# Dilated attention and a binary convolution on one core: four tiles for the weighted values, two softmax temporaries in one tile, two output tiles, and a subtraction moved within its slice

## The chip, the cores and the metric

The kernel runs on one core of a Trainium2 chip. The metric is the device time of one execution in microseconds (us). Engines are named as the profile names them: PE is TensorE (PEld its weight loads), DVE VectorE, ACT ScalarE, POOL GpSimd, SP SyncE, which here issues nearly all DMAs. Every compute engine and every DMA queue takes its instructions in one fixed order.

## The reference

The input x is 16 images of 56 x 56 pixels with 384 channels, float32. Two layers follow each other, each with a residual:

```python
def _gn(v, G=32, eps=1e-5):            # group norm over an image, 32 groups of 12 channels
    ...
# layer 0: three groups of 128 channels with dilation 1, 2, 3; 4 heads of 32 channels in each
q, k, v = split(einsum('bchw,oc->bohw', _gn(x), w_qkv))
attn = softmax(einsum('bgdn,bgdkn->bgnk', q, unfold(k)) * 32 ** -0.5)   # 9 neighbours of a pixel
y = einsum('bgnk,bgdkn->bgnd', attn, unfold(v))
x = x + einsum('bhwc,oc->bhwo', y, w_proj) + b_proj
# layer 1: depthwise 3x3 convolution with the signs of w
x = x + conv(_gn(x), sign(clip(w, -1, 1)))
```

So each pixel looks at nine neighbours at a distance of 1, 2 or 3, for 12 heads, and the result goes through a projection. The second layer needs the statistics of a whole image of the first.

## The kernel before

**Tiling.** An image is cut into 7 chunks of 8 rows (448 pixels); 112 chunks in all. Channels lie on the 128 partitions, pixels along the free dimension, so that one product is a [128, 448] float32 matmul and one [128, 3, 448] tile holds three neighbours. A tile of w takes 3 x 448 x 4 = 5376 bytes of each partition.

**Three plans.** plan_a loads a chunk of x, turns it to channels (L423), takes statistics and writes it to DRAM (xd). plan_b is the attention of chunk m. plan_c convolves the chunk ten steps earlier and writes the output. The pieces of these plans are put into a table with at(slice, order, piece): a chunk advances by 9 slices, and within a slice the pieces stand in the order SOFTMAX, SCORE, STATISTICS, CONVOLVE, WEIGH, QUERY, SPREAD, QKV, PROJECT, STAGE_A, STAGE_C, NORM, LOADS. The table is issued from front to back. The framework then fixes the order of each engine's instructions when it builds the program. It takes what is ready, and the issued order is a priority: in the trace, work of later slices stands ahead of earlier work in places. It also inserts every wait.

**The attention of a chunk**, with the names that the text below uses (t0 is 9m):
- project (L464) makes k and v in slices before and during the chunk, query the three q. The rows that chunks share are copied by small DMAs (L478, L479).
- score(i), slices t0 to t0+8: VectorE multiplies q with three neighbours of k into a tile t (L517), and TensorE adds over the channels of a head with a matrix of ones into ps (L502), in three bursts a chunk.
- softmax_1 (t0+9): ScalarE copies ps into the tile sT (L534), TensorE turns it to pixels (L537), VectorE subtracts the maximum (L540, L541), ScalarE takes the exponential (L542). softmax_2 (t0+10): VectorE's sum (L546), reciprocal, and product (L548).
- softmax_3 to 5: the float32 weights are split into three bf16 terms. ScalarE copies the first (L556, the tile e). GpSimd subtracts it from the weights into the tile rest (L560, softmax_4, slice t0+11), copies the second term (L564) and subtracts for the third (L565, softmax_5, slice t0+12). turn_weights is a transposing DMA into aT (L570) and needs all three.
- weigh(i), slices t0+14 to t0+22, i = 3g + ky: TensorE spreads the weights of three neighbours over the channels into pb_a (L583, one buffer of PSUM), VectorE multiplies them with v into a tile of w (L590), and for ky = 1 and 2 GpSimd adds that tile to the first of its group (L598). After ky = 2 GpSimd adds the three parts into y (L601, L602).
- out_project(j), slices t0+24 on (L616): it needs all three y.

Tiles of w come from the pool w_p, which has three; so a group's first tile stays in use until L602, and each of the other two until its own L598. The pool also gives out tiles for some chunks of the first image, and in every second chunk of the last image for the convolution's input (z_last).

**The convolution of a chunk** puts two thirds of the channels on TensorE (L711) and one third on ScalarE and GpSimd: the normalised tile zg (L740), nine products on ScalarE (L762), two big adds on GpSimd (L768, of [128, 1344]) and three small ones (L773, L773, L776). turn(s), four times a chunk, turns 112 pixels back (L783); ScalarE copies them into a tile osb (L788), and SP writes that to the output (L791). The pool o_p has three tiles of osb (1536 bytes of a partition each).

Of the kernel before, what the change touches and what calls it, by code (L numbers as in the profile page):

```python
# [8 lines left out]
F32 = mybir.dt.float32  # L9
# [8 lines left out]
P = 128  # L18
HEADS = 4
# [5 lines left out]
SUB = 112  # L25
# [3 lines left out]
NPAD = 32  # L29
# [6 lines left out]
def dilated_attention_then_binary_conv(  # L36
# [30 lines left out]
    PX = ROWS * W  # L67
    NCH = H // ROWS
    NSUB = PX // SUB
# [78 lines left out]
    xn_p = ctx.enter_context(tc.tile_pool(name="xn_p", bufs=3))  # L148
    xr_p = ctx.enter_context(tc.tile_pool(name="xr_p", bufs=1))
    t_p = ctx.enter_context(tc.tile_pool(name="t_p", bufs=4))  # L150
    w_p = ctx.enter_context(tc.tile_pool(name="w_p", bufs=3))
    y_p = ctx.enter_context(tc.tile_pool(name="y_p", bufs=4))
    s_p = ctx.enter_context(tc.tile_pool(name="s_p", bufs=1))
    a_p = ctx.enter_context(tc.tile_pool(name="a_p", bufs=2))
    x1_p = ctx.enter_context(tc.tile_pool(name="x1_p", bufs=2))
    xg_p = ctx.enter_context(tc.tile_pool(name="xg_p", bufs=2))
    m_p = ctx.enter_context(tc.tile_pool(name="m_p", bufs=3))
    o_p = ctx.enter_context(tc.tile_pool(name="o_p", bufs=3))


    kv = []
# [231 lines left out]
    def at(when, order, piece):  # L393

        pieces.setdefault((when, order), []).append(piece)
# [50 lines left out]
    def plan_b(m, t0):  # L446

        b, c = divmod(m, NCH)
        had = {}
# [75 lines left out]
        def by_neighbour(ap):  # L525
            return ap.rearrange("p s (o k) -> p s o k", o=NTAP)

        def over_neighbours(ap):
            return ap.unsqueeze(2).to_broadcast([SUB, NSUB, NTAP, GH])

        def softmax_1():

            sT = s_p.tile([P, PX], F32, tag="sT", name="sT")
            nc.scalar.copy(sT, had.pop("ps")[:, :PX])  # L534
            pt = ps_mt.tile([P, 512], F32, tag="mt", name="pt_s")
            for s in range(NSUB):
                nc.tensor.transpose(pt[:SUB, s * P : (s + 1) * P], sT[:, s * SUB : (s + 1) * SUB], permf)  # L537
            pt4 = pt[:SUB].rearrange("p (s v) -> p s v", s=NSUB)[:, :, :NR]
            mx = s_p.tile([SUB, NSUB, GH], F32, tag="mx", name="mx")
            nc.vector.reduce_max(mx, by_neighbour(pt4).rearrange("p s o k -> p s k o"), axis=AX.X)  # L540
            nc.vector.tensor_tensor(by_neighbour(weights), by_neighbour(pt4), over_neighbours(mx), ALU.subtract)  # L541
            nc.scalar.activation(weights, weights, AF.Exp, scale=SCALE)  # L542
# [13 lines left out]
            nc.scalar.copy(term[0], e8)  # L556

        def softmax_4():
            had["rest"] = rest = s_p.tile([SUB, NSUB * NPAD * HEADS], F32, tag="rest", name="rest")
            nc.gpsimd.tensor_tensor(rest.rearrange(EIGHTS, k=8), e8, term[0], ALU.subtract)  # L560

        def softmax_5():
# [70 lines left out]
        for i in range(9):  # L633
            at(t0 + i, SCORE, lambda i=i: score(i))
        at(t0 + 9, SOFTMAX, softmax_1)
        at(t0 + 10, SOFTMAX, softmax_2)
        at(t0 + 11, SOFTMAX, softmax_3)
        at(t0 + 11, PROJECT, softmax_4)
        at(t0 + 12, SOFTMAX, softmax_5)
        at(t0 + 12, LOADS, turn_weights)  # L640
        for i in range(9):
# [182 lines left out]
    SOFTMAX, SCORE, STATISTICS, CONVOLVE, WEIGH, QUERY, SPREAD, QKV, PROJECT, STAGE_A, STAGE_C, NORM, LOADS = range(13)  # L824
# [43 lines left out]
    for m in range(N):  # L868
        plan_a(m, start_a(m))
        plan_b(m, STEP * m)  # L870
        plan_c(m, STEP * (m + 10))
# [31 lines left out]
```

## Time and profile before

| | |
|---|---|
| median of 3 runs | 5359.44 us (5357.7 to 5360.04) |
| the profiled execution | 5363.24 us |
| its span, first to last instruction | 5361.5 us |
| mean granted TensorE clock | 0.978 |
| TensorE idle from 500 to 5000 us | 4500 less 4404.4 busy: 95.6 us |
| L598, GpSimd's add of w | 672 times, 3080 ns |
| L590, VectorE's product into w | 1008 times, 1543 ns |
| L560 / L564 / L565 on GpSimd | 112 times each, 1154 / 607 / 1159 ns |
| aT from issue to landing | 112 times, 4.0 us |
| output parts | 420 DMAs of 168 KB from tiles osb |

Busy time says how full an engine is over the whole span. Where an engine stands idle, the trace names what ended the wait: "PE ps L502 <- DVE t L517" means that TensorE's matmul into ps began when VectorE's product t was done. "L590 [1.93 <-POOL w L598]" means that VectorE had been idle for 1.93 us until GpSimd's add ended. "issue" is time in which the engine waited for nothing that the profile shows.

### The profile page before, as it was taken

What the parts mean: (1) busy time and instruction counts of PE and PEld (TensorE: products, weight loads), DVE (VectorE), ACT (ScalarE), POOL (GpSimd) and SP (SyncE); (2) the same over time, 40 slices, a digit from 0 to 9 for tenths busy, and PEclk for the clock granted to TensorE, in tenths of its full rate; (3) what the DMA queues carried; (4) which work ended last, traced back from release to release, by engine and by line L of the source; (5) the groups of instructions that cost most, each with busy time, mean ns of one, the idle gap of its engine ahead of it and who ended that gap; (6) DMA issues with size and microseconds to landing.
All of it is one profiled execution on the core that took longest, in us unless ns stands there. A gap on an engine that the chain in (4) does not pass through costs nothing. (4 is left out here: it accounts for less than half of the span.)

```text
span 5361.5 us, 75511 instructions
## 1 busy us (share of the span) xinstructions
PE 5146.8 (96%) x26885; PEld 2339.3 (44%) x26885; DVE 4173.9 (78%) x4125; ACT 2310.0 (43%) x4077; POOL 4254.0 (79%) x2950
## 2 busy tenths in 40 slices
PE   8999999999999999999999999999999999999976
PEld 4444444444444444444444444444444444444433
DVE  5887887778778777887878877777887878877764
ACT  3213444444444444444444444444434444444434
POOL 2777888888888887878888888888888888788881
PEclk8999999999999999999999999999999999999986
DMA  6434555555555555555555555565555555544455
GB/s 192 135 108 113 166 161 162 161 155 162 155 164 157 152 159 162 166 155 161 161 154 166 147 161 161 160 165 154 165 158 155 162 147 164 146 135 134 130 135 154
DMA packets 811631, 825.62 MB, mean 154 GB/s; under 512 B 360307, under 2 KB 801014, under 8 KB 811254
## 3 DMA queue, kind: packets, MB, share of 16 engines
q1 hardware_dynamic: 803270, 808.79, 54.7%
q10 hardware_dynamic: 7984, 12.00, 0.7%
q8 instruction: 213, 3.49, 0.3%
q14 instruction: 164, 1.34, 0.1%
HBM read 466.41 MB, written 231.21 MB: 130 GB/s over the span
## 5 line engine op out<-in xcount | busy, mean ns | idle before, releaser
L598 POOL TENSOR_TENSOR w<-w 128x1344 f32<-128x1344 f32 x672 | 2069.9, 3080 | 587.3 <-DVE w L590 544.6
L590 DVE TENSOR_TENSOR w<-pb_a,v 128x1344 f32<-128x1344 f32 x1008 | 1555.7, 1543 | 327.4 <-PE pb_a L583 213.9
L517 DVE TENSOR_TENSOR t<-pq,k 128x1344 f32<-128x1344 f32 x1008 | 1536.2, 1551 | 252.0 <-PE pq L464 251.6
L464 PE MATMUL pkv<-xn,wqkvT 128*128 128x448 f32 x3924 | 1567.6, 548 | 0.4 <-DVE xr L619 0.4
L464 PEld LDWEIGHTS pkv<-xn,wqkvT 128*128 128x128 f32 x3924 | 718.0, 190 | 670.7 <-issue 644.9
L464 PE MATMUL pq<-xn,wqkvT 128*128 128x448 f32 x1962 | 858.8, 573 | 0.0
L616 PE MATMUL po<-y,wprojT 128*128 128x448 f32 x2016 | 832.8, 549 | 23.9 <-POOL y L602 18.4
L697 ACT ACTIVATE z<-z,mrz 96x448 f32<-96x448 f32 x840 | 578.2, 751 | 631.6 <-DMA z<-x1d 371.5
L768 POOL TENSOR_TENSOR m<-m 128x1344 f32<-128x1344 f32 x210 | 640.1, 3048 | 147.4 <-ACT m L762 143.1
L502 PE MATMUL ps<-t,sel 128*32 128x448 f32 x6048 | 663.5, 548 | 45.0 <-DVE t L517 44.3
L762 ACT ACTIVATE m<-zg,ktap 128x448 f32<-128x448 f32 x945 | 555.5, 659 | 8.6 <-POOL xg L776 1.7
L616 PEld LDWEIGHTS po<-y,wprojT 128*128 128x128 f32 x2016 | 375.6, 191 | 381.5 <-issue 339.5
L711 PE MATMUL pc<-z,kdiag 96*32 96x440 f32 (+1 forms) x5040 | 517.5, 544 | 6.1 <-POOL z L699 4.4
L464 PEld LDWEIGHTS pq<-xn,wqkvT 128*128 128x128 f32 x1962 | 353.0, 194 | 330.3 <-issue 330.3
L583 PE MATMUL pb_a<-aT,spread 24*128 24x448 bf16 x3024 | 369.9, 360 | 82.6 <-DMA aT<-e 60.6
L602 POOL TENSOR_TENSOR y<-y,w 128x448 f32<-128x448 f32 x336 | 381.2, 1134 | 16.4
L601 POOL TENSOR_TENSOR y<-w 128x448 f32<-128x448 f32 x336 | 381.3, 1135 | 13.7
L619 DVE SCALAR_TENSOR_TENSOR xr<-po,bias,xr 128x448 f32<-128x448 f32 x336 | 227.9, 678 | 208.5 <-PE po L616 203.8
L474 ACT COPY v<-pkv 128x448 f32<-128x448 f32 x336 | 176.3, 525 | 493.7 <-PE pkv L464 484.7
L718 DVE TENSOR_TENSOR x<-pc,x 128x448 f32<-128x448 f32 x224 | 139.0, 621 | 310.4 <-PE pc L711 309.3
L583 PEld LDWEIGHTS <-spread 24*128 24x128 bf16 x3024 | 100.3, 91 | 571.1 <-issue 488.5
L474 ACT COPY k<-pkv 128x448 f32<-128x448 f32 x336 | 178.9, 532 | 377.2 <-PE pkv L464 377.2
(132 smaller groups left out, 4278.3 us busy)
## 6 DMA issues: line engine op xcount, KB each, us to landing
z<-x1d SPq DMA_DIRECT2D x570, 224.0 KB, 3.8
xr<-xd SPq DMA_DIRECT2D x112, 672.0 KB, 4.2
x1d<-xr SPq DMA_DIRECT2D x112, 672.0 KB, 3.2
xn<-xd SPq DMA_DIRECT2D x109, 672.0 KB, 4.6
xin<-in_x_dram SPq DMA_DIRECT2D x105, 672.0 KB, 7.2
xd<-xa SPq DMA_DIRECT2D x315, 224.0 KB, 3.3
out_dram<-osb SPq DMA_DIRECT2D x420, 168.0 KB, 3.5
x<-x1d SPq DMA_DIRECT2D x112, 448.0 KB, 8.1
```

What stands on the lines that cost most here:

```text
L464: nc.tensor.matmul(dst[:, :PX], wqkvT[:, cc, o0 : o0 + P], had["xn"][:, cc, :], start=(cc == 0), stop=(cc == NG - 1))
L502: return nc.tensor.matmul(had["ps"][32 * j : 32 * j + 32, :PX], sel[:, s0 : s0 + 32], tk, start=(issued[j] == 1), stop=(issued[j] == len(r ...
L517: nc.vector.tensor_tensor(t.rearrange("p k (r w) -> p k r w", w=W), q3, k3, ALU.mult)
L583: return nc.tensor.matmul(pb[:, kx, :PX].rearrange("p (s n) -> p s n", s=NSUB), spread[rows_of, v % 2, :], had["a"][rows_of, :, v // 8, :] ...
L590: nc.vector.tensor_tensor(w.rearrange("p k (r w) -> p k r w", w=W), pb[:, :, :PX].rearrange("p k (r w) -> p k r w", w=W), three(kv[1][g][m ...
L598: nc.gpsimd.tensor_tensor(w0, w0, w, ALU.add)
L601: nc.gpsimd.tensor_tensor(y, w0[:, 0], w0[:, 1], ALU.add)
L616: nc.tensor.matmul(po[:, :PX], wprojT[:, g, j * P : (j + 1) * P], had[f"y{g}"], start=(g == 0), stop=(g == NG - 1))
L697: nc.scalar.activation(z, z, AF.Identity, bias=mrz[:, j, q, 0:1], scale=mrz[:, j, q, 1:2])
L711: return nc.tensor.matmul(pcr[q * HD : (q + 1) * HD, :, lo:hi], kdiag[:, kx, j * NQ + q, :], rows(set_of(j, q))[:, :, lo + kx - 1 : hi + k ...
L762: nc.scalar.activation(rows(t[:, kx]), zp[:, ky : ky + ROWS, kx : kx + W], AF.Copy, scale=ktap[:, o : o + 1])
L768: nc.gpsimd.tensor_tensor(had["m"], had["m"], t, ALU.add)
```

## The change

The pool of w gets a fourth tile, and the pool of osb goes from three to two. The tile rest loses its own place: it takes the tag sT, of which there is one tile, now of 512 instead of 448 columns; so the turned scores and the rest share it in turns. In bytes of a partition: 5376 more for w, 1536 less for osb, 2048 less for rest, 256 more for sT, 2048 more in all. The piece softmax_4 stays in slice t0+11 but moves from the order PROJECT to SOFTMAX, behind softmax_3 of the same slice. No instruction's work changes.

```diff
-    w_p = ctx.enter_context(tc.tile_pool(name="w_p", bufs=3))
+    w_p = ctx.enter_context(tc.tile_pool(name="w_p", bufs=4))
...
-    o_p = ctx.enter_context(tc.tile_pool(name="o_p", bufs=3))
+    o_p = ctx.enter_context(tc.tile_pool(name="o_p", bufs=2))
...
-            sT = s_p.tile([P, PX], F32, tag="sT", name="sT")
+            sT = s_p.tile([P, NSUB * NPAD * HEADS], F32, tag="sT", name="sT")[:, :PX]
...
-            had["rest"] = rest = s_p.tile([SUB, NSUB * NPAD * HEADS], F32, tag="rest", name="rest")
+            had["rest"] = rest = s_p.tile([P, NSUB * NPAD * HEADS], F32, tag="sT", name="rest")[:SUB]
             nc.gpsimd.tensor_tensor(rest.rearrange(EIGHTS, k=8), e8, term[0], ALU.subtract)
...
-        at(t0 + 11, PROJECT, softmax_4)
+        at(t0 + 11, SOFTMAX, softmax_4)
```

## The prediction

> **What bounds the kernel now.** I read the page's busy line first. One engine is nearly full; the two behind it have a fifth of the span free.
>
> ```profile
> PE 5146.8 (96%) x26885; PEld 2339.3 (44%) x26885; DVE 4173.9 (78%) x4125; ACT 2310.0 (43%) x4077; POOL 4254.0 (79%) x2950
> ```
>
> So the end moves only if TensorE's idle time moves. It sums to some 210 us: 45 before 500 us, 96 in the regular part from 500 to 5000 us (4500 less 4404.4 busy, view by windows), 70 after it. Next comes the view of waits for 500 to 5000 us: who ended TensorE's idle time, and VectorE's (in total us, times, longest).
>
> ```profile
> PE pb_a L583 <- DMA aT<-e: 48.8, 13, 4.0
> PE ps L502 <- DVE t L517: 36.6, 36, 1.5
> PE po L616 <- ACT v L474: 5.2, 8, 2.1
> PE pb_a L583 <- DVE w L590: 3.9, 12, 0.4
> ...
> DVE w L590 <- POOL w L598: 47.8, 35, 3.9
> ```
>
> Two causes make nearly all of it. TensorE waits for the turned weights aT 13 times, once per image. And it waits for VectorE's score products t, 1 us at a time. The last line offers a reason for the second: VectorE itself stands before a product w until GpSimd has finished an addition. The timeline of chunk 48 shows whether the two belong together (start, duration, then what is idle in brackets).
>
> ```profile
> 2311.63 2.37 POOL L773 TENSOR_TENSOR m<-m 128x448 f32<-128x448 f32 x2
> 2314.08 1.14 POOL L776 TENSOR_TENSOR xg<-m,xg 128x448 f32<-128x448 f32 x1
> 2315.17 3.03 POOL L598 TENSOR_TENSOR w<-w 128x1344 f32<-128x1344 f32 x1
> ```
> ```profile
> 2313.72 0.36 PE L583 MATMUL pb_a<-aT,spread 24*128 24x448 bf16 x3
> ...
> 2319.85 0.37 PE L583 MATMUL pb_a<-aT,spread 24*128 24x448 bf16 x3 [0.34 <-DVE w L590]
> ...
> 2322.14 1.33 PE L502 MATMUL ps<-t,sel 128*32 128x448 f32 x12 [1.46 <-DVE t L517]
> ```
> ```profile
> 2315.71 0.59 DVE L541 TENSOR_TENSOR ew<-pt_s,mx 112x432 f32<-112x432 f32 x1
> 2318.24 1.56 DVE L590 TENSOR_TENSOR w<-pb_a,v 128x1344 f32<-128x1344 f32 x1 [1.93 <-POOL w L598]
> 2319.71 0.91 DVE L546 TENSOR_REDUCE sm<-ew 112x48 f32<-112x432 f32 x1
> 2320.54 1.55 DVE L517 TENSOR_TENSOR t<-pq,k 128x1344 f32<-128x1344 f32 x1
> ```
>
> This is one chain. The convolution's adds (L768, L773, L776) stand ahead of L598, so the sum of weigh(2) ends at 2318.2. Only then is one of three tiles of w free for weigh(4), whose input pb_a was ready at 2314.1. Its product starts 1.93 us after VectorE had become free, the sum sm and the product t follow it, and TensorE loses 0.34 and 1.46 us. I went through every such gap in 500 to 5000 us: in 31 gaps before ps (35.5 us) and 12 before pb_a (3.9 us) a wait of a w for L598 lies within the 9 us before. Per image it is weigh(4) of the last chunk and of the first.
>
> **What the Trainium skill says.** Perfetto Trace Analysis, Optimization Strategy: the same gap repeating on the engine that should be saturated can mean that there isn't enough SBUF for the next tile. The trace agrees: the 1.46 us above recurs image after image behind a tile that isn't free. SBUF — State Buffer, Who interferes with whom: a VectorE instruction with two SBUF inputs contends with GpSimd's reads, one with a single SBUF input does not. The trace agrees: L548 (two SBUF inputs) takes 583 to 2611 ns, L590 (one PSUM, one SBUF input) 1482 to 1560. So products w that run earlier, beside GpSimd's adds, should not grow.
>
> **The change, part by part.**
>
> *Fourth tile of w.* No instruction is added. weigh(4) may then start when VectorE is free, at 2316.3; sm's sum follows at 2317.8 (its input, the exponential, was there at 2317.0), t at 2318.6 to 2320.2. TensorE is through with its transposes at 2320.35 (2320.69 less the 0.34), so ps waits for nothing: 1.80 us gained. Summed over the regular part: 35.5 + 3.9 = 39.4 us. From below: the skipped wait returns where GpSimd is late next. That is y into the output projection (L602 of chunk 48 ended 2342.6, its first use comes some 5 us later) and aT. For aT I looked at the landing against the first weigh: in ordinary chunks 11.2 us after the end of the bf16 copy L556, against 13.9 when TensorE gets there, so 2.7 us of slack. TensorE comes 1.8 us earlier, GpSimd's chain 0.9 (its idle time before the sum of weigh(5) at 2324.53): 1.8 us of slack stay. I take the whole 39.4; the lower bound is a half, 20.
> Before 500 us the same pattern is worth 0.3 + 2.4 = 2.7 us. From 5000 to 5230 us 13.1 us of TensorE's gaps stand behind such waits, but GpSimd is busy 204.4 of these 230 us and the two waits for y (10.7 and 7.7 us) come from it; only its own idle time before a sum (2.0 + 0.7 + 1.1 us) can go. I take 3, between 0 and 4. The last image's z_last tiles also come from this pool in every second chunk; the chunks between use the four tiles of t and show the same 3.8 us gap, so the tiles don't set it. I take 0, between -4 and 2.
>
> *The rest in the tile of the turned scores.* It adds two orders: L560 after the transposes of sT, and the next chunk's copy L534 after L565. In chunk 48 the transposes were over at 2313.8, L560 began at 2327.8; L565 ended at 2332.8 and the next L534 began at 2355.8. Slacks of 14 and 23 us: nothing. If they were gone, ScalarE would hold its queue (copies of v, k, xa) for the time missing.
>
> *Two output parts.* ScalarE's copy of part n+2 now waits until part n has landed. The view of the tile osb gives the DMA itself:
>
> ```profile
> DMA to landing us min/median/max: 2.1/3.5/5.3
> ```
>
> Taking each copy's landing (where the trace doesn't link one, 3.5 us after its issue) against the start of the copy two later, the order of before leaves over 0.25 us in every case but two of 418, both near 5213 us (3.0 and 0.3 us), where GpSimd is the bound. Price 0; at most 3.3 us; more only if another order packs three copies closely (below).
>
> *Subtraction first in its slice.* softmax_4 issues one instruction, L560 (1.15 us), and no DMA, so SP's queue is passed by nothing. On GpSimd it moves past what its slice holds between the two places: the convolution's second big add (L768, 3.05 us) and, once per image, L333 and L334 (0.19 + 0.20 us). In the trace L768 has run before that point anyway, and L560 stands ahead of L333. Behind L560 on GpSimd are y's adds and L565, which aT and then TensorE wait for. Nothing in the regular order changes: 0. The bound above is the aT wait. Chunk 44 shows it:
>
> ```profile
> 2098.51 1.13 POOL L773 TENSOR_TENSOR m<-m 128x448 f32<-128x448 f32 x1
> 2099.60 1.13 POOL L601 TENSOR_TENSOR y<-w 128x448 f32<-128x448 f32 x1
> 2100.69 1.15 POOL L560 TENSOR_TENSOR rest<-ew,e 112x512 f32<-112x512 f32 x1
> ...
> 2104.56 1.16 POOL L565 TENSOR_TENSOR e<-rest,e 112x512 bf16<-112x512 f32 x1
> ```
>
> L560's input was ready at 2095.2; it starts 5.5 us later, and TensorE loses 3.96 us. But this L773 belongs to a chunk whose zg was made at 2075 us, and its slice is 4 or more after L560's; it still stands ahead: the order is made when the program is built, by what is ready then, and a place within the slice doesn't make L560 ready sooner. I take 0; up to 48.8 us if the builder places it otherwise; down to a loss of its wait for L556 before a ready add, 1.15 us a chunk at most in the chunks without slack.
>
> The sum: 39.4 + 2.7 + 3 + 0 = 45.1 us. The profiled execution took 5363.24 us (span 5361.5 and 1.7 around it), which gives 5318.1; the median of the runs lies 3.8 below that execution, so 5314.3.
>
> **The rivals.**
> *A. Slower: VectorE runs too far ahead.* With a fourth tile a product w (1.55 us, not interruptible) can be placed ahead of a score product t that TensorE wants sooner. The builder re-makes the whole order. Place: the three bursts of ps in each chunk. Price: up to 1.55 us for each burst hit; at 0.8 us once per chunk, 112 x 0.8 = 90 us, less the 45 gained: 5404. It decides from 45.1 / 0.8 = 56 chunks on. For it: already now TensorE loses 0.2 us before ps in several chunks where no w waited, so VectorE is just in time. Against: pb_a has one PSUM buffer, which limits the lead to one product past TensorE's own order.
> *B. The subtraction gets ahead in the third chunk of each image.* Then the 48.8 us go too: 5314.3 - 48.8 = 5265.5. For it: L560 was ready 5 us before its turn. Against: the readiness argument above.
> *C. Nothing gained.* The two-part output or GpSimd hands the time back: products start earlier, but TensorE then waits for aT or y by the same amount. 5359. Against: the slacks of 1.8 and 5 us.
> That the fourth tile isn't used would show as C too.
>
> **How the numbers follow.** Forecast 0.50 (own range 5298 to 5338), B 0.12, C 0.10, A 0.28. About 0.2% (10.7 us) is what a measurement of this kernel can tell from no change. Faster: 0.50 + 0.12 = 0.62; same 0.10; slower 0.28. The range runs from 5275 to 5405: it leaves out B's centre and the upper half of A, under 0.2 together.
>
> **What would show it.** Right: in 500 to 5000 us the line of w waiting for POOL w falls from 47.8 to under 10 us, ps waiting for t from 36.6 to under 8, pb_a waiting for aT stays near 49; busy times are unchanged. Wrong: ps waiting for t grows (A); aT falls to near 0 (B); aT, y, or ScalarE's osb waiting for its own DMA grows by what ps lost (C).

## The result and the profile after

| | before | after |
|---|---|---|
| median, same chip | 5359.74 us (5357.7 to 5362.44, 4 runs) | 5321.87 us (5315.76 to 5325.16, 4 runs) |
| the profiled execution | 5363.24 us (span 5361.5) | 5322.62 us (span 5320.9) |
| mean granted TensorE clock | 0.978 | 0.980 |
| TensorE busy / idle over the span | 5146.8 / 214.7 us | 5132.4 / 188.5 us |

The change makes the kernel faster: ratio 0.9928, 95% interval 0.9911 to 0.9945, 37.9 us by the medians. The busy line of the page after:

```profile
PE 5132.4 (96%) x26885; PEld 2336.6 (44%) x26885; DVE 4203.7 (79%) x4125; ACT 2312.1 (43%) x4077; POOL 4255.0 (80%) x2950
```

The instruction counts are those of before. TensorE has 14 us less busy time for the same work, which the paragraph on the sum takes up. The view of waits from 500 to 5000 us, TensorE's lines and VectorE's for GpSimd (total us, times, longest):

```profile
PE pb_a L583 <- DMA aT<-e: 50.7, 14, 4.0
PE po L616 <- ACT v L474: 11.7, 17, 2.0
PE po L616 <- POOL y L602: 3.7, 1, 3.7
PE ps L502 <- DVE t L517: 1.5, 7, 0.2
...
DVE w L590 <- POOL m L768: 11.3, 8, 1.4
DVE w L590 <- POOL e L564: 10.8, 12, 0.9
```

VectorE's 47.8 us for "POOL w" are gone, and with them TensorE's 36.6 us for t (1.5 left) and 3.9 us for w. The wait for aT stays; its 14th occurrence, 1.7 us at 4973 us, is one that the shorter kernel brings into the window. Two lines have grown: v on ScalarE from 5.2 to 11.7 us, and one wait for y of 3.7 us, at 500.5 us.

Chunk 48 again, the timeline after, first GpSimd, then VectorE and TensorE:

```profile
2298.08 2.37 POOL L773 TENSOR_TENSOR m<-m 128x448 f32<-128x448 f32 x2
2300.53 1.13 POOL L776 TENSOR_TENSOR xg<-m,xg 128x448 f32<-128x448 f32 x1
2301.61 3.04 POOL L598 TENSOR_TENSOR w<-w 128x1344 f32<-128x1344 f32 x1
```
```profile
2302.35 0.59 DVE L541 TENSOR_TENSOR ew<-pt_s,mx 112x432 f32<-112x432 f32 x1
2302.86 1.55 DVE L590 TENSOR_TENSOR w<-pb_a,v 128x1344 f32<-128x1344 f32 x1
2304.32 0.91 DVE L546 TENSOR_REDUCE sm<-ew 112x48 f32<-112x432 f32 x1
2305.14 1.56 DVE L517 TENSOR_TENSOR t<-pq,k 128x1344 f32<-128x1344 f32 x1
```
```profile
2306.85 1.71 PE L502 MATMUL ps<-t,sel 128*32 128x448 f32 x16
```

GpSimd's order is as before, and L598 still ends late, at 2304.65. But the product L590 starts at 2302.86, 1.8 us ahead of that, because it writes the fourth tile. t follows in time, and the burst into ps has no bracket behind it. TensorE's sequence of matmuls, by line and tile, is the same in both traces from the first to the last of 26885. So the two can be laid over each other, matmul by matmul: after less before is -7 us at 500, but within 0.5 us of nothing both at 480 and at 520, then -12 at 2000, -22 at 3000, -33 at 4000, -41 at 5000 and -41 at the end. The gain grows image by image in the regular part; the start and the tail add nothing.

### The profile page after: what moved, and what is told of

Read it like the earlier page. It is cut to its first block, busy times and chain, and to the rows that moved or that the text cites. A ratio compares the mean times of both kernels' runs of the same rounds, so it can differ in the third digit from the quotient of the medians.

```text
span 5320.9 us, 75544 instructions
## 1 busy us (share of the span) xinstructions
PE 5132.4 (96%) x26885; PEld 2336.6 (44%) x26885; DVE 4203.7 (79%) x4125; ACT 2312.1 (43%) x4077; POOL 4255.0 (80%) x2950
## 5 line engine op out<-in xcount | busy, mean ns | idle before, releaser
L598 POOL TENSOR_TENSOR w<-w 128x1344 f32<-128x1344 f32 x672 | 2071.2, 3082 | 535.1 <-DVE w L590 510.4
L590 DVE TENSOR_TENSOR w<-pb_a,v 128x1344 f32<-128x1344 f32 x1008 | 1555.1, 1543 | 276.6 <-PE pb_a L583 225.3
L616 PE MATMUL po<-y,wprojT 128*128 128x448 f32 x2016 | 841.0, 553 | 44.0 <-POOL y L602 32.1
L768 POOL TENSOR_TENSOR m<-m 128x1344 f32<-128x1344 f32 x210 | 640.2, 3048 | 148.2 <-ACT m L762 144.3
```

The source lines that it names most:

```text
L590: nc.vector.tensor_tensor(w.rearrange("p k (r w) -> p k r w", w=W), pb[:, :, :PX].rearrange("p k (r w) -> p k r w", w=W), three(kv[1][g][m ...
L598: nc.gpsimd.tensor_tensor(w0, w0, w, ALU.add)
L616: nc.tensor.matmul(po[:, :PX], wprojT[:, g, j * P : (j + 1) * P], had[f"y{g}"], start=(g == 0), stop=(g == NG - 1))
L768: nc.gpsimd.tensor_tensor(had["m"], had["m"], t, ALU.add)
```

## The experiments

Each was run beside the kernel before. The theory: the fourth tile makes the whole gain, by taking away VectorE's wait for a tile of w; the other edits only make room for it or do nothing; the wait for aT is a second cost that GpSimd's order makes.

**e1: the change with three tiles of w.**

```diff
-    w_p = ctx.enter_context(tc.tile_pool(name="w_p", bufs=4))
+    w_p = ctx.enter_context(tc.tile_pool(name="w_p", bufs=3))
```

> The changed kernel with three tiles of w again: two output parts, the shared tile and the moved subtraction stay. Theory (the fourth tile is the whole gain, the rest is worth nothing): 5360 us within 6, as before the change; from 500 to 5000 us ps waits for t some 36 us and w for POOL w some 48. Rival (the other edits, which alter the order of the last chunks and ScalarE's queue, bring part of it): below 5350, and with all of it near 5322.

Measured: 5359.52 us, ratio to before 1.0008 (0.9999 to 1.0017). Waits from 500 to 5000 us:

```profile
PE ps L502 <- DVE t L517: 34.3, 35, 1.5
...
DVE w L590 <- POOL w L598: 43.6, 33, 4.0
```

Both waits are back, and with them the whole time. Without the fourth tile the other three edits together are worth nothing. The fourth tile without them was not run, so whether it needs the room that they make is not shown.

**e8: the moved subtraction alone, on the kernel before.**

```diff
-        at(t0 + 11, PROJECT, softmax_4)
+        at(t0 + 11, SOFTMAX, softmax_4)
```

> The kernel before with the moved subtraction alone (softmax_4 with the order SOFTMAX). Theory (the builder's choice rests on what is ready, and the place within the slice changes no engine's order): the ratio to before is 1.000, within 0.001, and pb_a waits for aT 47 to 51 us. Rival (B of the prediction: the subtraction gets ahead of L773 in the third chunk of each image): aT near 10 us and some 5308 us.

Measured: 5360.53 us, ratio 1.0000 (0.9992 to 1.0009). The wait for aT is 49.0 us, as before. Every engine's order is that of before (two weight loads apart), so this run is also a second sample of the same program. Its span is 5351.5 us against 5361.5: one profiled execution tells such a program's time to some 10 us only.

**e3: the change with one output part.**

```diff
-    o_p = ctx.enter_context(tc.tile_pool(name="o_p", bufs=2))
+    o_p = ctx.enter_context(tc.tile_pool(name="o_p", bufs=1))
```

> The changed kernel with one output part instead of two; ScalarE's and SP's order change with it. Set against the changed kernel's own times, each copy but one in two would have to wait up to 5 us for the landing of the part before it (197 of 419 copies, 768 us in all on ScalarE). Theory (with two parts the landing is covered, with one it isn't, and ScalarE's queue then reaches TensorE through the copies of k and v): clearly slower than the changed kernel, 5400 to 5700. Rival (ScalarE has the room, 43% busy, and the order is remade around the waits): within 15 us of 5322; then the number of output parts costs nothing at all in this kernel.

Measured: 5413.17 us, ratio 1.0106 (1.0089 to 1.0122), some 90 us above the kernel after. Waits from 500 to 5000 us, TensorE's and one of ScalarE's:

```profile
PE pb_a L583 <- DVE w L590: 33.4, 30, 2.2
PE po L616 <- ACT v L474: 26.3, 40, 1.7
PE pc L711 <- ACT osb L788: 24.0, 12, 3.2
...
ACT osb L788 <- DMA out_dram<-osb: 424.7, 137, 6.8
```

ScalarE stands until a part has landed, and the copies behind it are late. In the kernel after, ScalarE waits so only once, 4.5 us at 5173 us, in the tail. So two are enough, and one is not.

**e5: three tiles, and the convolution's small adds moved behind the sum.** This asks whether the tile or GpSimd's order was the cause. On the kernel before, with `behind(ins, piece)` issuing a piece so that it stands behind `ins` in its engine's queue:

```diff
-            nc.gpsimd.tensor_tensor(w0, w0, w, ALU.add)
+            second[m, i] = nc.gpsimd.tensor_tensor(w0, w0, w, ALU.add)
...
-            at(t0 + 5 + kx, CONVOLVE, lambda kx=kx: sum_g(kx))
+            at(t0 + 5 + kx, CONVOLVE, lambda kx=kx: behind(second.get((m + 8, 2)) if c >= 5 else None, lambda: sum_g(kx)))
```

> The kernel before, three tiles of w, one edit: in the last two chunks of an image of the convolution (c 5 and 6) the three small adds L773, L773, L776 are issued behind L598 of weigh(2) of the attention's chunk m+8, ahead of which they stood. Orders of TensorE, VectorE and ScalarE stay as before but for the last chunks; GpSimd's alone changes. Theory (the tile of w is late because these 3.5 us of adds stand ahead of L598; a fourth tile only hides that): VectorE's wait for POOL w falls from 47.8 us to under 12, ps waiting for t from 36.6 to under 10, aT stays at 48 to 52; 5319 us (5312 to 5330), as with the fourth tile. Rival (three tiles are too few whatever GpSimd's order, since it is some 80% busy and another add will be late): the waits stay over 25 us and the time is 5340 to 5362.

Measured: 5323.47 us, ratio 0.9928 (0.9912 to 0.9945), the ratio of the change itself.

```profile
PE pb_a L583 <- DMA aT<-e: 50.7, 14, 4.0
PE po L616 <- ACT v L474: 9.3, 12, 2.1
PE ps L502 <- DVE t L517: 1.8, 8, 0.3
...
DVE w L590 <- POOL w L598: 8.7, 4, 3.9
```

The chain of the prediction is shown from its other end: with the 3.5 us of L773, L773 and L776 out of the way of L598, three tiles do what four do. The tile buys patience with an order; the order can be had without the tile.

**e2: the change, with the adds of an image's first chunk of the convolution behind L565.** This is what rival B would have brought.

```diff
-            nc.gpsimd.tensor_tensor(term[2], r8, term[1], ALU.subtract)
+            third[m] = nc.gpsimd.tensor_tensor(term[2], r8, term[1], ALU.subtract)
...
-            at(t0 + 5 + kx, CONVOLVE, lambda kx=kx: sum_g(kx))
+            at(t0 + 5 + kx, CONVOLVE, lambda kx=kx: behind(third.get(m + 9) if c == 0 else None, lambda: sum_g(kx)))
```

> The changed kernel, with the three small convolution adds (L773 twice, L776) of each image's first chunk held behind L565 of the chunk in whose slices they fall; TensorE's and VectorE's order stay. Theory (aT is late once per image because 3.4 us of convolution adds and the sum of weigh(5) stand ahead of L560 and L565): TensorE's wait for aT falls from 50.7 us to 10 or less from 500 to 5000 us, some 3.3 us in each of 15 images, and the time from 5322 to 5275 (5265 to 5290). Rival 1 (the held adds make the convolution's output or y late instead): aT falls but the time stays above 5305. Rival 2 (aT is late through its DMA or SP's queue, not through GpSimd's order): aT stays near 50 and the time near 5322.

Measured: 5272.7 us (5269.0 to 5275.65), ratio 0.9844 (0.9829 to 0.9859): the fastest version of the study, 85 us below before. Waits, and GpSimd in chunk 44:

```profile
PE po L616 <- ACT v L474: 21.8, 27, 1.5
PE pb_a L583 <- DMA aT<-e: 10.4, 14, 1.8
```
```profile
2068.57 1.18 POOL L560 TENSOR_TENSOR rest<-ew,e 112x512 f32<-112x512 f32 x1
2069.69 1.15 POOL L601 TENSOR_TENSOR y<-w 128x448 f32<-128x448 f32 x1
...
2072.44 1.17 POOL L565 TENSOR_TENSOR e<-rest,e 112x512 bf16<-112x512 f32 x1
2073.55 2.38 POOL L773 TENSOR_TENSOR m<-m 128x448 f32<-128x448 f32 x2
```

L773 now stands behind L565. The wait for aT falls by 40.3 us, v takes 10.1 of them back, and yet the span falls by 53.6 us (5320.9 to 5267.3). The rest is busy time of TensorE, 23 us less of it, and goes with the clock (below).

**e6 and e9: is the fourth tile needed for that?** e6 puts e2's edit on the kernel before; e9 puts the edits of e2 and e5 there, both with three tiles.

> The kernel before, three tiles of w, with the edit of e2_sums_behind alone: the adds L773, L773, L776 of an image's first chunk of the convolution issued behind L565 of chunk m+9. Theory (the two waits are in different chunks of an image and have nothing to do with each other): the same 49 us as it gave with four tiles, 5357 - 49 = 5308 us (5300 to 5318); pb_a waiting for aT falls from 48.8 to some 10, ps waiting for t stays at 33 to 38, the ratio is 0.991. Rival (they share GpSimd's slack, so the adds put off come to lie ahead of an L598 that has only three tiles): the wait of VectorE for POOL w grows over 60 us and the time is 5325 to 5350.

Measured: 5326.09 us, ratio 0.9933 (0.9918 to 0.9948), the rival's range.

```profile
PE ps L502 <- DVE t L517: 46.0, 45, 1.5
PE po L616 <- ACT v L474: 20.6, 21, 2.4
PE pb_a L583 <- DMA aT<-e: 11.9, 14, 1.8
...
DVE w L590 <- POOL w L598: 98.0, 57, 4.1
```

The wait for aT goes, but VectorE's wait for a tile doubles: the adds put off now stand ahead of an L598 of the third chunk. TensorE pays 9.4 us of it before ps, and its wait for v grows by 15.4 us (5.2 to 20.6) besides.

> The kernel before, three tiles of w, with both edits: those of e5_order_three and of e2_sums_behind (sums of c 5 and 6 behind L598 of chunk m+8's weigh(2), sums of c 0 behind L565 of chunk m+9). Theory (e6 fell short because the adds put off come to lie ahead of an L598 in the third chunk, a gap of 1.07 us before ps once in each of 13 images that only a fourth tile hides): ps waiting for t is 12 to 18 us, aT some 10 us, VectorE's wait for POOL w 40 to 60 us, and the ratio to before is 0.987 (0.9855 to 0.9885), some 14 us over e2_sums_behind. Rival (the two orders together leave no late tile, three are as good as four): the ratio of e2_sums_behind, 0.984 to 0.9854, and ps waiting for t under 6 us.

Measured: 5286.9 us, ratio 0.9859 (0.9844 to 0.9873).

```profile
PE ps L502 <- DVE t L517: 13.8, 19, 1.1
PE pb_a L583 <- DMA aT<-e: 12.9, 14, 1.8
...
DVE w L590 <- POOL w L598: 59.8, 27, 4.1
```

The ratio, ps and VectorE's wait lie in the theory's intervals, the last just so. A gap of some 1.1 us before ps in the third chunk recurs in 10 images of the trace. So the fourth tile does all that e5's order does, and where e2's order is used it seems to be worth more: 12 us less wait before ps than in e9 (2.0 against 13.8), 8 us by the ratios, whose intervals overlap.

**e4: y's adds of the last three chunks on VectorE**, aimed at the waits for y after 5000 us.

```diff
-                nc.gpsimd.tensor_tensor(y, w0[:, 0], w0[:, 1], ALU.add)
-                nc.gpsimd.tensor_tensor(y, y, w0[:, 2], ALU.add)
+                (nc.vector if m >= N - 3 else nc.gpsimd).tensor_tensor(y, w0[:, 0], w0[:, 1], ALU.add)
+                (nc.vector if m >= N - 3 else nc.gpsimd).tensor_tensor(y, y, w0[:, 2], ALU.add)
```

> The changed kernel with the adds into y (L601, L602) of the last three chunks on VectorE instead of GpSimd: 18 adds of 1.13 us leave GpSimd. Theory (the fourth tile brings nothing after 5000 us because GpSimd bounds the last three chunks): TensorE's wait for y falls from 28.5 us there to under 12 and the time by 8 to 18 us, to 5304 to 5314. Rival (the end is set by the loads of z_last and TensorE's lower clock): within 4 us of 5322.

Measured: 5339.73 us, ratio 0.9967 (0.9957 to 0.9978), about 20 us above the kernel after. Both expectations missed. VectorE's and TensorE's waits from 4900 us on:

```profile
DVE y L601 <- POOL w L598: 36.6, 8, 9.2
```
```profile
PE pb_a L583 <- DVE w L590: 31.7, 10, 6.3
PE po L616 <- DVE y L602: 17.6, 2, 10.0
```

The add needs GpSimd's last L598. On GpSimd's own queue that order costs nothing; on VectorE's, the next products w and t are queued behind a wait of up to 9.2 us. The adds themselves are longer there too: the 18 take 22.0 us, where 0.61 us each, the shortest of them, would make 11. How the loss divides between the two, this run doesn't show.

**e7 and e10: the copies of v.** They are what grew in e2. Here is ScalarE, and then TensorE, in the last chunk of an image, in the kernel after:

```profile
3610.81 2.72 ACT L697 ACTIVATE z<-z,mrz 96x448 f32<-96x448 f32 x4 [7.01 <-DMA out_dram<-osb]
3614.12 0.81 ACT L740 ACTIVATE zg<-xg,mr 128x504 f32<-128x504 f32 x1 [0.59 <-DMA xg<-x1d]
3614.96 4.03 ACT L762 ACTIVATE m<-zg,ktap 128x448 f32<-128x448 f32 x7
3618.89 0.52 ACT L474 COPY v<-pkv 128x448 f32<-128x448 f32 x1
```
```profile
3619.46 2.08 PE L616 MATMUL po<-y,wprojT 128*128 128x448 f32 x3 [2.05 <-ACT v L474]
```

ScalarE stood for 7 us until a DMA had landed (the trace names an output part's; the loads of z and xg are in the same queue of SP). The copy of v is behind all of it, and until it has read pkv, TensorE has no free PSUM tile of that pool for po. e7 issues the loads of the convolution's inputs one slice earlier, on top of e2:

```diff
-        at(t0 - 4, LOADS, load_g)
+        at(t0 - 5, LOADS, load_g)
...
-            at(t0 - 4 + 3 * j, LOADS, lambda j=j: load(j))
+            at(t0 - 5 + 3 * j, LOADS, lambda j=j: load(j))
```

> e2_sums_behind with the loads of the convolution's inputs (L684, L703, L729) issued one slice, some 5 us, earlier. TensorE's order and ScalarE's change with it from an early point on, so this is not one wait taken away alone. Theory (the copies of v on ScalarE are late because z and zg ahead of them stand for these loads): po waiting for ACT v falls from 21.8 us to under 10, and 5272 becomes 5260 (5252 to 5268). Rival (the loads wait in SP's queue behind aT's issue wherever they are issued, or ScalarE is late for another reason): within 4 of 5272. A second rival: loads ahead of aT's issue in SP's queue hold that back, aT grows by 10 us or more and the time is 5280 or above.

Measured: ratio 0.9847 (0.9831 to 0.9863), 5277.8 us, no different from e2; v costs 32.1 us, where the theory had under 10. Over the whole run ScalarE's idle time before z fell from 664.7 to 578.6 us, but before xn, whose load shares SP's queue, it rose from 52.4 to 205.0. The wait moved. e10 takes the output parts from that queue instead:

```diff
-            queue = nc.sync if b < B - 1 else nc.scalar
+            queue = nc.scalar
```

> e2_sums_behind with the output parts (L791, 420 DMAs, 0.4 us each to issue on SP) issued by ScalarE, which has just copied them, in place of SP. TensorE's order stays but for the last chunks. Theory (SP's one queue makes the loads of z and xg late, z and zg hold ScalarE, and the copies of v behind them hold TensorE): po waiting for ACT v falls from 21.8 us to under 12 and the ratio to before goes from 0.9844 to 0.982 (0.981 to 0.983). Rival (ScalarE pays for the 420 issues, 420 x 0.4 = 168 us in its queue, some of it ahead of copies that TensorE waits for): po or ps or pb_a waits longer for ACT, ratio 0.985 to 0.992.

Measured: 5370.25 us, ratio 1.0018 (1.0011 to 1.0025), over 90 us slower than e2. The theory missed; it is the rival's mechanism, beyond its price:

```profile
PE po L616 <- ACT v L474: 82.0, 66, 2.8
PE pb_a L583 <- DMA aT<-e: 23.4, 14, 2.0
```

The order of ScalarE's copies and taps changed with the 420 issues. How much of the loss is the issues' own time and how much the new order, these runs don't separate.

**e11 and e12: the clock.** The profile records the clock granted to TensorE, which is 1 or 0.5 in these traces. In 500 to 5000 us the records show 0.5 for 3.4 or 6.8 us behind each of the 12 long waits for aT, in the kernels before and after, and behind none of e2's shorter ones. The pq matmuls behind the wait show it, before:

```profile
2109.83 0.56 PE L583 MATMUL pb_a<-aT,spread 24*128 24x448 bf16 x3 [3.96 <-DMA aT<-e]
2110.32 3.35 PE L464 MATMUL pq<-xn,wqkvT 128*128 128x448 f32 x4
```

e11 and e12 fill the wait with 7 or 3 needless matmuls; shown is e11:

```diff
-            in_one_go([lambda kx=kx: copy(kx) for kx in (2, 0, 1)])
+            in_one_go([lambda k=k: nc.tensor.matmul(pb[:, k % 3, :PX], wqkvT[:, 0, :P], wqkvT[:, 0, :PX], start=True, stop=True) for k in range(7 if c == 2 and i == 0 and 2 <= b <= 13 else 0)] + [lambda kx=kx: copy(kx) for kx in (2, 0, 1)])
```

> The kernel after, with 7 more float32 matmuls of 128x448 ahead of weigh(0)'s copies in the third chunk of images 2 to 13, into the tile pb_a that those copies then overwrite: work that nobody needs, some 2.8 us, in each of the 12 waits for aT of 3.9 us. TensorE's order is otherwise that of after. The wait itself ends when it did. Theory (each such wait costs more than its 3.9 us: the records show a granted clock of 0.5 for 3.4 or 6.8 us behind each of the 12, in sum 54 us, so 27 us of work lost): the clock lost from 500 to 5000 us falls from 34 us to under 10, pb_a waiting for aT from 50.7 us to 13 to 20, and the time from 5322 to 5297 us (5292 to 5306), a ratio to before of 0.988. Rival (the records of the clock don't bear on the time, the wait is the whole cost): 5322 us within 4, a ratio of 0.992 to 0.9935. A second rival: the added matmuls hold back the copies behind them: 5330 us and more.

> As e11_fill_gap with 3 added matmuls, some 1.2 us, so that TensorE stands for 2.7 us in each of the 12 waits. If what counts is a single long wait[...], this is as good as 7: 5297 us (5292 to 5306). If any idle time of over 2 us in a short stretch slows the clock, as once behind a wait of 2.05 us in the kernel after, half or more of the loss stays: 5307 to 5322 us.

Measured: 5336.73 us, ratio 0.9952 (0.9938 to 0.9965), with 7, and 5336.16 us, 0.9954 (0.9941 to 0.9966), with 3: both slower than the kernel after, where the theory wanted 25 us less. The added matmuls were mis-sized: each leaves two records of some 0.4 us in a row (168 for the 84 of e11), so 7 take about 5.5 us, more than the wait, and 3 take 2.5. In e11 the second rival's price, 5330 us and more, is what came out; in e12 both forecasts missed. The clock did as the theory says. What half speed took from 500 to 5000 us (half of the time spent at it) fell from 34 us to 10 and 12. e12 in chunk 44:

```profile
2097.68 2.52 PE L588 MATMUL pb_a<-wqkvT 128*128 128x448 f32 x6
2101.68 0.37 PE L583 MATMUL pb_a<-aT,spread 24*128 24x448 bf16 x3 [1.47 <-DMA aT<-e]
2101.98 2.52 PE L464 MATMUL pq<-xn,wqkvT 128*128 128x448 f32 x6
```

Six such records take 2.52 us at each of e12's 12 waits. In the kernel after they take 4.05 to 4.85, 4.40 on average: 12 x 1.9 = 23 us. That a long wait slows the work behind it is shown. That a filler pays is not, because the program built around it has another order on ScalarE. In chunk 44 four taps instead of none stand between z and v:

```profile
2110.78 2.70 ACT L697 ACTIVATE z<-z,mrz 96x448 f32<-96x448 f32 x4
2113.39 2.33 ACT L762 ACTIVATE m<-zg,ktap 128x448 f32<-128x448 f32 x4
2115.62 0.52 ACT L474 COPY v<-pkv 128x448 f32<-128x448 f32 x1
```

TensorE then waits 1.77 us for v there, and from 500 to 5000 us 39.0 us (28.2 in e11) against 11.7 after:

```profile
PE po L616 <- ACT v L474: 39.0, 31, 3.1
```

A filler with ScalarE's order held was not tried.

## Why the prediction was right, and where it was off

**The step that carries it held.** Of 35.5 + 3.9 us of gaps behind a late tile, TensorE's lines for t and w show 39.0 us gone (36.6 and 3.9 to 1.5 and nothing). e1 shows that it is the fourth tile, e5 that the cause was the three adds ahead of L598.

**"I take the whole 39.4" was too much.** From 520 to 5000 us the overlay of the two traces gains 40.5 us, but only 34 of them are TensorE's idle time, which is what the 39.4 stood for. The prediction looked for what is late next at y and aT. aT was right: its slack held. ScalarE was not looked at: po waiting for v took 6.5 us back, in the last chunks of an image, where v stands behind z, zg and the taps. This is the term that was missing: 39.0 - 6.5 = 32.5. The other 7 us are shorter busy time, which goes with the clock: in this stretch half speed took 37.5 us before and 30.7 after. Whether the change brings any of that is open: from 500 to 5000 us it is 38.0 before and 34.1 after, but 37.5 in e4, whose orders are those of after up to 5000 us.

**Before 500 us** 2.7 us were taken, and nothing came. The 7.3 us that the kernel after is ahead at 500 us are a moment's: what a wait for w of 2.4 us and a stretch of half speed beside it cost the kernel before, the wait for y of 3.7 us and half speed behind it cost the kernel after, and at 520 us 0.4 us are left. y's slack of some 5 us was read in the regular part and does not hold at the start.

**The tail was put at 3 (0 to 4) and gave nothing.** Waits for y after 5000 us grew from 18.4 to 28.5 us: GpSimd is the bound there, and TensorE, 41 us ahead, only waits longer. All its idle time in the tail grew by 9 us, and 9 us less busy time made up for it.

```profile
PE po L616 <- POOL y L602: 28.5, 4, 11.3
```

**The sum.** Of 45.1 us the profiled execution shows 40.6: 26.2 of idle time, which alone the prediction had in it, and 14.4 of busy time. About 13 of the latter are the clock: by its records half speed took 117.8 us of the whole span before and 104.6 after. In e8, the program of before, it took 107.8, so 10 us of this differ between two executions of one program and are not counted to the change. That the total came so near to the forecast is in part luck: of the idle time a little over half of what was forecast went. The medians give 37.9.

**What was priced at nothing was nothing.** e8 shows it for the moved subtraction, and the argument by readiness was right. Two output parts and the shared tile cost nothing: e1 has both and equals before.

**The rivals.** A did not happen: ps waiting for t is 1.5 us. C happened for a part, through v. B did not come by this change, but e2 shows its place to be real. Its 48.8 us (from after to e2 45 by the ratios, 53.6 by the profiled executions) were about right by two errors that cancel: a part of the wait stays (10.4 us) and v takes 10 back, while the end of the long waits frees 23 us of half-speed work (busy 5132.4 to 5109.3 us) that the price left out.

## What to carry to other kernels

Where an engine waits for a buffer, look at what stands ahead of the instruction that frees it: a further buffer and another order can be worth the same, and the order costs no memory. Before a wait is credited to the total, ask every engine in the loop what its slack is, the half-empty ones too: a copy at the end of an in-order queue has no slack although its engine is 43% busy. An operation moved to a freer engine takes its wait along, and all that is queued there pays for it.

## What the runs showed of the hardware

A long wait of TensorE costs more than its length. The Trainium skill, TensorE: Matmul & The Clock Gate, HAM oscillation — how this bites in real kernels, says that idle gaps over about 3.4 us bring the clock to half and that it must warm up again. The traces agree, with 3.9 us waits and 4.40 instead of 2.52 us for the six records behind. They also show shorter ones that do it: 2.05 us before po at 3617.4 us in the kernel after was followed by half clock from 3620.0 on, and 1.79 us at 4662.0 from 4664.5 on, while e12's 12 shortened waits for aT, 1.5 to 2.2 us, were not, nor its wait of 2.74 us before po at 824.2 us. In the kernel before, even three of the waits for t, 1.2 us each, were followed by half clock (at 2691, 3988 and 4637 us); in e8, with the same program, it was five, of 1.17 to 1.46 us, four of them at other places. So among the shorter ones the program alone doesn't decide; what does stays open. The mean clock says it in short, 0.980 after and here e2:

```profile
core 0: 5267.3 us, clock 0.985
```

Busy time less the time lost to the clock is 5029, 5028 and 5029 us for before, after and e2 (5146.8 - 117.8, 5132.4 - 104.6, 5109.3 - 80.4), and 5026 to 5042 us in the other nine runs without added matmuls: the records of the clock account for the difference in busy time to 1 us in these three, and to some 15 us over all.

In e4 an add of y with both inputs in SBUF took VectorE 0.62 us alone and 3.3 to 3.5 us beside GpSimd's L768. That agrees with the passage of the Trainium skill, SBUF — State Buffer, Who interferes with whom, that the prediction draws on.
